# Four-layer graph stack: runs of three pairs of heads, a ring of row sums, and another close of each block in the multi-head layer

## The chip, the cores and the metric

The kernel runs on one core of a Trainium2 chip. The metric is the device time of one execution in microseconds. Before the change three runs took 3386.57, 3389.37 and 3391.87 us; the median is 3389.37.

## The reference

Four graph layers follow each other on 4096 nodes with 256 features. Each is a kind of masked attention, whose output is added to its input and normalised by row. `adj` is a 4096 x 4096 matrix of 0 and 1. The change touches only layer 1, the multi-head one:

```python
x = _layernorm(x + _L0_gnn_ref(x, adj, W, a))            # additive, 4 heads
x = _layernorm(x + _L1_gnn_ref(x, adj, Wq, bq, ...))     # multi-head, 4 heads of 64
x = _layernorm(x + _L2_gnn_ref(x, adj, W, a))            # additive, 1 head
x = _layernorm(x + _L3_gnn_ref(x, adj, Wq, Wk))          # cosine

def _L1_gnn_ref(x, edge, Wq, bq, Wk, bk, Wv, bv):
    q, k, v = (_split_heads(x @ W + b) for W, b in ...)  # 4 heads of 64
    mask = (edge.T.astype(jnp.float32) - 1.0) * 10000.0
    scores = jnp.einsum('hnd,hmd->hnm', q, k) / np.sqrt(64)
    attn = jax.nn.softmax(scores + mask[None], axis=-1)
    ctx = jnp.einsum('hnm,hmd->hnd', attn, v)
    return ctx.transpose(1, 0, 2).reshape(x.shape[0], 256)
```

So each head needs the products of its exponentials with V, and their sums over m (the row sums), by which the products are divided.

## The kernel before

Everything is in 32-bit floats, and X, the features, stays in SBUF. The four layers are written one after another; `multi_head_attention` (L276 to L427) is the second. It first makes kT, qT (features on partitions) and V (nodes on partitions), then works through 8 blocks b of 512 output nodes. In a block it goes through 32 tiles j of 128 source nodes. In a step the scores lie transposed: source nodes on partitions, 512 outputs along the free axis.

The four heads go in two pairs, c = 0 and 1; r is the head within a pair. The two heads of a pair lie on partitions 0 to 63 and 64 to 127 of kT and qT. `weights` (L348) does this for a j, for both pairs: two score matmuls (L361), each contracting over 64 rows of the PE array, into a PSUM tile p of two banks; the exponential on ScalarE in place (L363); the multiplication by the mask on VectorE into an SBUF tile `prob` (L365); and the addition of `prob` to a running sum `den` in SBUF (L372, L374). Pair 0 is added by GpSimd in part 0. Pair 1 is added by VectorE in part 1, but for every fourth j, which GpSimd adds in part 2. `sums` (L376) multiplies `prob` by V (L383): two matmuls a pair with 64 output columns each, which go to the two halves of the PE array and accumulate in a PSUM tile `acc` over all 32 j. After the last j `acc` is copied out as `accS`, one half by ScalarE (L387), one by VectorE (L388).

`outputs` (L390) closes a block: matmuls of `den` with one column of ones sum over the partitions (24 of them, L398), their reciprocals are taken (L401), `accS` is transposed back by eight transposes (L405), multiplied by the reciprocals (L407) and added to X (L412), and `row_stats` takes mean and variance of each row for the layer norm (L101, L102).

The order is written out by hand at L416 to L425: `weights` of a step, then `sums` of the step before it, and the close of a block after step j = 1 of the next one. The tile framework turns the accesses into semaphore waits and keeps each engine's queue in nearly that order. A tile of a pool comes free when the last reader of its buffer is done. [...]three tiles p of two banks (`mh_pz`) and one `acc` of two (`mh_pa`). The tiles of the close, for row sums and transposes, are taken from the same three buffers p. Masks come by SP's queue as 32-bit integers, four tiles j in a load of 1 MB, three buffers. There are four `prob` buffers.

Of the kernel before, what the change touches and what calls it, by code (L numbers as in the profile page):

```python
# [8 lines left out]
FP = mybir.dt.float32  # L9
BF = mybir.dt.bfloat16  # L10
I32 = mybir.dt.int32
AF = mybir.ActivationFunctionType
OP = mybir.AluOpType
AX = mybir.AxisListType
PSUM = bass.MemoryType.PSUM

P = 128
D = 256
KC = D // P
QB = 4  # L20
QW = QB * P
# [5 lines left out]
def kernel(  # L27
# [25 lines left out]
    nc = tc.nc  # L53
    N = x.shape[0]
    NT = N // P
    NB = N // QW
# [4 lines left out]
    ident = const.tile([P, P], FP, name="ident")  # L61
# [42 lines left out]
    def finish_stats():  # L104
        nc.scalar.activation(rstd, stats[:, :, 1], AF.Sqrt, bias=eps)
        nc.vector.reciprocal(rstd, rstd)

    def normalise(y, t):
        nc.vector.tensor_scalar(y, y, stats[:, t, 0:1], rstd[:, t:t + 1], OP.subtract, OP.mult)  # L109

    def layernorm():
        finish_stats()
        for t in range(NT):
            normalise(X[:, t, :D], t)


    def additive_attention(w, a_src, a_dst, H, slope):
# [4 lines left out]
        g = 1.0 - slope  # L122
        MJ = 4
        with ExitStack() as lay:
# [48 lines left out]
            def weights(b, j):  # L173
                m = b, j // MJ
                if j % MJ == 0:
                    mask[m] = mp.tile([P, MJ, QW], I32, name="mask")
                    nc.sync.dma_start(mask[m], edges[:, j:j + MJ, b * QW:(b + 1) * QW])
                e = sb.tile([P, H, QW], FP, name="e")
                for h in range(H):
                    nc.scalar.activation(e[:, h, :], row[b][:, h, :], AF.Relu, bias=-1.0, scale=dst[:, j, h:h + 1])  # L180
                z = prob[b, j] = zp.tile([P, H, QW], FP, name="prob")
                nc.vector.scalar_tensor_tensor(z, e, 1.0, mask[m][:, j % MJ, :].unsqueeze(1).to_broadcast([P, H, QW]),  # L182
                                               OP.add, OP.mult)
# [75 lines left out]
            units = [(b, j) for b in range(NB) for j in range(NT)]  # L259
            LAG = 1  # L260
            for i in range(len(units) + LAG):
                if i < len(units):
                    b, j = units[i]
                    weights(b, j)
                    if H > 1 and j == NT // 2 and b + 1 < NB:
                        rows(ps, b + 1)
                if i >= LAG:
                    b, j = units[i - LAG]
                    sums(b, j)
# [6 lines left out]
    def multi_head_attention():  # L276
# [2 lines left out]

        H = 4  # L280
        d = D // H
        MJ = 4
        with ExitStack() as lay:
            keep = lay.enter_context(tc.tile_pool(name="mh_keep", bufs=1))
            kT = keep.tile([P, KC, N], FP, name="kT")
            qT = keep.tile([P, KC, N], FP, name="qT")
            V = keep.tile([P, NT, D], FP, name="V")
            ones = keep.tile([P, P], FP, name="ones")
            nc.vector.memset(ones, 1.0)
            shift = keep.tile([P, 1], FP, name="shift")  # L290
            qscale = d ** -0.5

            with tc.tile_pool(name="mh_w", bufs=1) as wp, \
# [10 lines left out]
                for b in range(NB):  # L304
                    xT = transposed_block(sb, ps, b)
                    for n, to, scale in (("k", kT, 1.0), ("q", qT, qscale)):
                        for o in range(KC):
                            pk = ps.tile([P, QW], FP, name="pk")
                            for c in range(KC):
                                nc.tensor.matmul(pk, w_sb[n][:, c, o * P:(o + 1) * P], xT[:, c, :],  # L310
                                                 start=(c == 0), stop=(c == KC - 1))
                            part = to[:, o, b * QW:(b + 1) * QW]
# [3 lines left out]
                    for k in range(QB):  # L316
                        pv = ps.tile([P, D], FP, name="pv")
                        for c in range(KC):
                            nc.tensor.matmul(pv, xT[:, c, k * P:(k + 1) * P], w_sb["v"][:, c, :],
                                             start=(c == 0), stop=(c == KC - 1))  # L320
# [9 lines left out]
                for r in range(KC):  # L330
                    half = slice(r * d, (r + 1) * d)
# [4 lines left out]
                nc.vector.tensor_scalar(shift, shift, -1.0, ROOM, OP.mult, OP.add)  # L336
                nc.vector.tensor_scalar_min(shift, shift, 0.0)

            sb = lay.enter_context(tc.tile_pool(name="mh_sb", bufs=4))
            mp = lay.enter_context(tc.tile_pool(name="mh_mask", bufs=3))  # L340
            ap = lay.enter_context(tc.tile_pool(name="mh_acc", bufs=1))
            dp = lay.enter_context(tc.tile_pool(name="mh_den", bufs=2))
            ps = lay.enter_context(tc.tile_pool(name="mh_pz", bufs=3, space=PSUM))
            pa = lay.enter_context(tc.tile_pool(name="mh_pa", bufs=1, space=PSUM))
            edges = adj.rearrange("(t p) i -> p t i", p=P)
            mask, acc, prob, den = {}, {}, {}, {}

            def weights(u):  # L348
                b, j = u
                cols = slice(b * QW, (b + 1) * QW)  # L350
                m = b, j // MJ
                if j % MJ == 0:
                    mask[m] = mp.tile([P, MJ, QW], I32, name="mask")
                    nc.sync.dma_start(mask[m], edges[:, j:j + MJ, cols])
                if j == 0:
                    den[b] = dp.tile([P, 3, KC * QW], FP, name="den")
                for c in range(KC):
                    p = ps.tile([P, KC, QW], FP, name="p")
                    for r in range(KC):
                        half = slice(r * d, (r + 1) * d)  # L360
                        nc.tensor.matmul(p[:, r, :], kT[half, c, j * P:(j + 1) * P], qT[half, c, cols],  # L361
                                         start=True, stop=True)
                    nc.scalar.activation(p, p, AF.Exp, bias=shift)  # L363
                    z = prob[b, j, c] = sb.tile([P, KC, QW], FP, name="prob")
                    nc.vector.tensor_tensor(z, p, mask[m][:, j % MJ, :].unsqueeze(1).to_broadcast([P, KC, QW]),  # L365
                                            OP.mult)

                    part, eng = (0, nc.gpsimd) if c == 0 else (2, nc.gpsimd) if j % 4 == 3 else (1, nc.vector)
                    to = den[b][:, part, :]
                    flat = z.rearrange("p r i -> p (r i)")  # L370
                    if j == 0 or (part == 2 and j == 3):
                        eng.tensor_copy(to, flat)  # L372
                    else:
                        eng.tensor_tensor(to, to, flat, OP.add)  # L374

            def sums(u):  # L376
                b, j = u
                if j == 0:
                    acc[b] = pa.tile([P, KC, QW], FP, name="acc")
                for c in range(KC):  # L380
                    for r in range(KC):
                        h = KC * c + r
                        nc.tensor.matmul(acc[b][r * d:(r + 1) * d, c, :], V[:, j, h * d:(h + 1) * d],  # L383
                                         prob[b, j, c][:, r, :], start=(j == 0), stop=(j == NT - 1))
                if j == NT - 1:
                    s = acc[b, "sb"] = ap.tile([P, KC, QW], FP, name="accS")
                    nc.scalar.copy(s[:, 0, :], acc[b][:, 0, :])  # L387
                    nc.vector.tensor_copy(s[:, 1, :], acc[b][:, 1, :])  # L388

            def outputs(b):  # L390
                s = acc[b, "sb"]
                pd = ps.tile([P, QB, H], FP, name="p")
                for k in range(QB):
                    for h in range(H):
                        lo = (h % KC) * QW + k * P
                        parts = (0,) if h < KC else (1, 2)
                        for n in parts:
                            nc.tensor.matmul(pd[:, k, h:h + 1], den[b][:, n, lo:lo + P], ones[:, 0:1],  # L398
                                             start=(n == parts[0]), stop=(n == parts[-1]))
                rden = ap.tile([P, QB, H], FP, name="rden")  # L400
                nc.vector.reciprocal(rden, pd)  # L401
                po = ps.tile([P, QB, D], FP, name="p")
                for k in range(QB):
                    for c in range(KC):
                        nc.tensor.transpose(po[:, k, c * P:(c + 1) * P], s[:, c, k * P:(k + 1) * P], ident)  # L405
                o = ap.tile([P, QB, D], FP, name="o")
                nc.vector.tensor_tensor(o.rearrange("p k (h d) -> p (k h) d", h=H),  # L407
                                        po.rearrange("p k (h d) -> p (k h) d", h=H),
                                        rden.rearrange("p k h -> p (k h)").unsqueeze(2).to_broadcast([P, QB * H, d]),
                                        OP.mult)  # L410
                y = X[:, b * QB:(b + 1) * QB, :D]
                nc.vector.tensor_tensor(y, y, o, OP.add)  # L412
                for k in range(QB):
                    row_stats(sb, X[:, b * QB + k, :D], b * QB + k)

            units = [(b, j) for b in range(NB) for j in range(NT)]  # L416
            LAG = 1
            for i in range(len(units) + LAG):
                if i < len(units):
                    weights(units[i])  # L420
                if i >= LAG:
                    u = units[i - LAG]
                    sums(u)
                    if u[1] == 1 and u[0]:
                        outputs(u[0] - 1)  # L425
            outputs(NB - 1)
            layernorm()  # L427


# [139 lines left out]
```

## Time and profile before

| | us |
|---|---|
| median of three runs | 3389.37 |
| profiled execution | 3383.42 |
| its span | 3381.6 |
| multi-head layer, main loop, from the first L361 to the last L383 | 990.6 to 2043 |
| PE busy / VectorE / ScalarE / GpSimd over the span | 95% / 65% / 50% / 32% |
| in 1380 to 1500 us: PE / VectorE / ScalarE / GpSimd busy of 120 us | 118.8 / 104.2 / 59.4 / 96.7 |
| granted TensorE clock, mean | 0.976 |

A 32-bit matmul stands as two records in the trace, so an "x8" in the timeline is four matmuls of the program. Matmuls of different row or column groups of the PE array run at the same time. A row of a group gives the busy time and the mean of one instruction in ns; behind the second bar stands the idle time of the engine ahead of these instructions, and who ended it.

### The profile page before, as it was taken

The page shows a single profiled execution, that of the slowest core. Times are in us where ns is not written, and L with a number is a line of the kernel's source. Part 1 is how long each engine was busy: PE and PEld are TensorE (multiplying, and loading weights), DVE is VectorE, ACT ScalarE, POOL GpSimd, SP SyncE. Part 2 cuts the span into 40 slices and gives each one's busy share as a digit, 9 for nine tenths or more (in the row PEclk, how much of TensorE's full clock was granted, in tenths as well). Part 3 has the DMA queues.
Part 4 walks back from the last instruction along what each step waited for, and adds up shares of the span by engine and source line. Part 5 has one row for each costly group of instructions (what it writes and reads, how often), then busy time and mean ns, then how long its engine had stood idle before and what let it go on. Part 6 is the DMA issues. An engine that isn't in the chain of part 4 may idle for free. (4 is left out here: it accounts for less than half of the span.)

```text
span 3381.6 us, 37876 instructions
## 1 busy us (share of the span) xinstructions
PE 3226.4 (95%) x14596; PEld 1608.3 (48%) x14596; DVE 2201.5 (65%) x2738; ACT 1687.3 (50%) x2589; POOL 1067.1 (32%) x486
## 2 busy tenths in 40 slices
PE   7999999999799999999999997999997899999997
PEld 4222222222342332333333324788886677777775
DVE  4777887778559889888898895444545433333333
ACT  4888888888335455454454552444443422222221
POOL 0011111011019788797797892001101000000000
PEclk9999999999899999999999997999998999999998
DMA  3222222222101111121121111344442233333332
GB/s 106 88 88 75 88 88 76 87 88 75 49 13 63 63 63 64 62 75 63 51 74 63 63 50 44 112 144 142 143 144 78 37 51 50 50 50 50 51 52 60
DMA packets 146965, 247.93 MB, mean 73 GB/s; under 512 B 5344, under 2 KB 48480, under 8 KB 146784
## 3 DMA queue, kind: packets, MB, share of 16 engines
q1 hardware_dynamic: 109824, 209.73, 19.0%
q0 software_dynamic: 33280, 33.56, 6.5%
q8 instruction: 114, 1.87, 0.2%
q10 hardware_dynamic: 3680, 2.23, 0.2%
q14 instruction: 67, 0.55, 0.1%
HBM read 274.86 MB, written 4.19 MB: 83 GB/s over the span
## 5 line engine op out<-in xcount | busy, mean ns | idle before, releaser
L182 DVE SCALAR_TENSOR_TENSOR prob<-e,mask 128x2048 f32<-128x2048 f32 (+1 forms) x512 | 765.7, 1496 | 364.6 <-PE acc L215 213.5
L374 POOL TENSOR_TENSOR den<-den,prob 128x1024 f32<-128x1024 f32 x304 | 864.0, 2857 | 167.0 <-DVE prob L365 155.8
L363 ACT ACTIVATE p<-p,shift 128x1024 f32<-128x1024 f32 x512 | 537.6, 1085 | 501.7 <-PE p L361 501.7
L180 ACT ACTIVATE e<-row,dst 128x512 f32<-128x512 f32 x1024 | 657.7, 711 | 77.7 <-DVE prob L182 77.7
L365 DVE TENSOR_TENSOR prob<-p,mask 128x1024 f32<-128x1024 f32 x512 | 601.7, 1214 | 79.9 <-issue 67.3
L361 PE MATMUL p<-qT,kT 64*128 64x512 f32 x2048 | 523.2, 627 | 13.6 <-DVE prob L365 13.2
L238 PE MATMUL acc<-prob,V 128*64 128x512 f32 x2048 | 528.8, 608 | 0.0
L383 PE MATMUL acc<-prob,V 128*64 128x512 f32 x2048 | 496.7, 606 | 0.1
L491 PE MATMUL acc<-X,prob 128*128 128x257 f32 x2048 | 487.0, 382 | 4.0 <-DVE prob L484 4.0
L491 PEld LDWEIGHTS acc<-X,prob 128*128 128x128 f32 x2048 | 389.5, 191 | 165.5 <-issue 112.4
L215 PE MATMUL acc<-V,prob 128*128 128x257 f32 x2048 | 450.0, 381 | 18.0 <-DVE prob L182 17.0
L192 POOL TENSOR_SCALAR neg<-o 128x256 f32<-128x256 f32 x64 | 57.5, 899 | 1278.2 <-DVE o L189 753.3
L484 DVE TENSOR_TENSOR prob<-prob,mask 128x512 f32<-128x512 f32 x256 | 176.2, 691 | 437.2 <-ACT prob L483 427.2
L215 PEld LDWEIGHTS acc<-V,prob 128*128 128x128 f32 x2048 | 386.9, 190 | 80.9 <-DVE prob L182 25.5
L483 ACT ACTIVATE prob<-p 128x512 f32<-128x512 f32 x256 | 152.2, 597 | 513.4 <-PE p L480 464.6
L361 PEld LDWEIGHTS p<-qT,kT 64*128 64x128 f32 x2048 | 177.6, 189 | 347.8 <-issue 300.0
L374 DVE TENSOR_TENSOR den<-den,prob 128x1024 f32<-128x1024 f32 x184 | 301.8, 1640 | 6.1
L238 PEld LDWEIGHTS acc<-prob,V 128*64 128x64 f32 x2048 | 128.9, 136 | 354.2 <-issue 204.8
L180 ACT ACTIVATE e<-allrows,dst 128x512 f32<-128x512 f32 x256 | 184.1, 721 | 223.0 <-DVE prob L182 221.2
L383 PEld LDWEIGHTS acc<-prob,V 128*64 128x64 f32 x2048 | 124.3, 136 | 344.2 <-issue 321.5
L241 PE MATMUL acc<-prob,V 128*32 128x512 f32 x2048 | 278.9, 604 | 0.0
L480 PE MATMUL p<-kT,qT 128*128 128x512 f32 x512 | 259.6, 592 | 0.7 <-ACT kT L465 0.7
(111 smaller groups left out, 1549.2 us busy)
## 6 DMA issues: line engine op xcount, KB each, us to landing
mask<-in_adjT SPq DMA_DIRECT2D x128, 1024.0 KB, 5.2
mask<-in_adj SPq DMA_DIRECT2D x64, 1024.0 KB, 5.2
mask<-in_adjT POOLq DMA_DIRECT2D x32, 1024.0 KB, 8.5
X<-in_x SPq DMA_DIRECT2D x8, 512.0 KB, 9.5
out<-Y SPq DMA_DIRECT2D x8, 512.0 KB, 4.0
w_sb<-in_w ACTq DMA_DIRECT2D x2, 256.0 KB, 4.9
a<-in_a ACTq DMA_DIRECT2D x4, 128.0 KB, 8.0
wq_sb<-in_wq ACTq DMA_DIRECT2D x1, 256.0 KB, 2.7
```

The source lines that it names most:

```text
L180: nc.scalar.activation(e[:, h, :], row[b][:, h, :], AF.Relu, bias=-1.0, scale=dst[:, j, h:h + 1])
L182: nc.vector.scalar_tensor_tensor(z, e, 1.0, mask[m][:, j % MJ, :].unsqueeze(1).to_broadcast([P, H, QW]), OP.add, OP.mult)
L215: nc.tensor.matmul(acc[b][k], prob[b, j][:, 0, k * P:(k + 1) * P], V[:, j, :], start=(j == 0), stop=(j == NT - 1))
L238: nc.tensor.matmul(acc[b][lo:lo + d, h // 2, :], V[:, j, h * d:(h + 1) * d], prob[b, j][:, h, :], start=(j == 0), stop=(j == NT - 1))
L241: nc.tensor.matmul(acc[b][h * G:(h + 1) * G, HC, :], V[:, j, D + h:D + h + 1].to_broadcast([P, G]), prob[b, j][:, h, :], start=(j == 0), s ...
L361: nc.tensor.matmul(p[:, r, :], kT[half, c, j * P:(j + 1) * P], qT[half, c, cols], start=True, stop=True)
L363: nc.scalar.activation(p, p, AF.Exp, bias=shift)
L365: nc.vector.tensor_tensor(z, p, mask[m][:, j % MJ, :].unsqueeze(1).to_broadcast([P, KC, QW]), OP.mult)
L374: eng.tensor_tensor(to, to, flat, OP.add)
L383: nc.tensor.matmul(acc[b][r * d:(r + 1) * d, c, :], V[:, j, h * d:(h + 1) * d], prob[b, j, c][:, r, :], start=(j == 0), stop=(j == NT - 1))
L480: nc.tensor.matmul(p, T["q"][:, j * P:(j + 1) * P], T["k"][:, cols], start=True, stop=True)
L491: nc.tensor.matmul(acc[b][k], prob[u][:, k * P:(k + 1) * P], X[:, j, :], start=(j == 0), stop=(j == NT - 1))
```

## The change

Only `multi_head_attention` changes.

- The unit of the order is now one pair (b, j, c) instead of both pairs of a j. Units go in runs of three: scores of three units, then sums of the three units of the run before, so that PE changes between scores and sums after six matmuls of the program instead of four.
- The row sums: pair 0, and pair 1 of odd j, are added by GpSimd to the two parts of `den`. Pair 1 of even j is not added one by one: its `prob` is written into a slot of a ring tile with three slots. After j = 2, 6, 10, ... one VectorE `tensor_reduce` sums the slots into slot 0 of the next ring tile (two buffers). Slot 0 carries the sum, and slots 1 and 2 take the next two units.
- The close: the row sums over partitions are now six matmuls with 32 output columns and 512 elements each, a group of 32 partitions for each head, copied out by ScalarE (`denS`) and transposed by four transposes. The result of the division goes into `accS` again instead of a tile of its own. It comes after the sums of unit j = 2 of the next block, and the row statistics only after j = 6. Both halves of `accS` are copied by ScalarE.
- Buffers: masks come two tiles j in a load (512 KB) instead of four, `prob` has five buffers, and a tile of the pool `mh_sb` two.

```diff
@@ -279,7 +279,7 @@
         H = 4
         d = D // H
-        MJ = 4
+        MJ = 2
         with ExitStack() as lay:
             keep = lay.enter_context(tc.tile_pool(name="mh_keep", bufs=1))
             kT = keep.tile([P, KC, N], FP, name="kT")
@@ -336,94 +336,121 @@
                 nc.vector.tensor_scalar(shift, shift, -1.0, ROOM, OP.mult, OP.add)
                 nc.vector.tensor_scalar_min(shift, shift, 0.0)
-            sb = lay.enter_context(tc.tile_pool(name="mh_sb", bufs=4))
+            sb = lay.enter_context(tc.tile_pool(name="mh_sb", bufs=2))
+            zp = lay.enter_context(tc.tile_pool(name="mh_z", bufs=5))
+            rp = lay.enter_context(tc.tile_pool(name="mh_ring", bufs=2))
             mp = lay.enter_context(tc.tile_pool(name="mh_mask", bufs=3))
             ap = lay.enter_context(tc.tile_pool(name="mh_acc", bufs=1))
             dp = lay.enter_context(tc.tile_pool(name="mh_den", bufs=2))
             ps = lay.enter_context(tc.tile_pool(name="mh_pz", bufs=3, space=PSUM))
             pa = lay.enter_context(tc.tile_pool(name="mh_pa", bufs=1, space=PSUM))
             edges = adj.rearrange("(t p) i -> p t i", p=P)
-            mask, acc, prob, den = {}, {}, {}, {}
-
-            def weights(u):
-                b, j = u
+            mask, acc, prob, den, ring = {}, {}, {}, {}, {}
+            W = KC * QW
+            RJ = 4
+            def weights(b, j, c):
                 cols = slice(b * QW, (b + 1) * QW)
                 m = b, j // MJ
-                if j % MJ == 0:
+                if c == 0 and j % MJ == 0:
                     mask[m] = mp.tile([P, MJ, QW], I32, name="mask")
                     nc.sync.dma_start(mask[m], edges[:, j:j + MJ, cols])
-                if j == 0:
-                    den[b] = dp.tile([P, 3, KC * QW], FP, name="den")
-                for c in range(KC):
-                    p = ps.tile([P, KC, QW], FP, name="p")
-                    for r in range(KC):
-                        half = slice(r * d, (r + 1) * d)
-                        nc.tensor.matmul(p[:, r, :], kT[half, c, j * P:(j + 1) * P], qT[half, c, cols],
-                                         start=True, stop=True)
-                    nc.scalar.activation(p, p, AF.Exp, bias=shift)
-                    z = prob[b, j, c] = sb.tile([P, KC, QW], FP, name="prob")
-                    nc.vector.tensor_tensor(z, p, mask[m][:, j % MJ, :].unsqueeze(1).to_broadcast([P, KC, QW]),
-                                            OP.mult)
-
-                    part, eng = (0, nc.gpsimd) if c == 0 else (2, nc.gpsimd) if j % 4 == 3 else (1, nc.vector)
-                    to = den[b][:, part, :]
+                if c == 0 and j == 0:
+                    den[b] = dp.tile([P, 2, W], FP, name="den")
+                p = ps.tile([P, KC, QW], FP, name="p")
+                for r in range(KC):
+                    half = slice(r * d, (r + 1) * d)
+                    nc.tensor.matmul(p[:, r, :], kT[half, c, j * P:(j + 1) * P], qT[half, c, cols],
+                                     start=True, stop=True)
+                nc.scalar.activation(p, p, AF.Exp, bias=shift)
+                ringed = c == 1 and j % 2 == 0
+                if ringed:
+                    if j == 0:
+                        ring[b, 0] = rp.tile([P, 3, W], FP, name="ring")
+                    flat = ring[b, j // RJ][:, 1 + (j % RJ) // 2, :]
+                    z = flat.rearrange("p (r i) -> p r i", r=KC)
+                else:
+                    z = zp.tile([P, KC, QW], FP, name="prob")
                     flat = z.rearrange("p r i -> p (r i)")
-                    if j == 0 or (part == 2 and j == 3):
-                        eng.tensor_copy(to, flat)
+                prob[b, j, c] = z
+                nc.vector.tensor_tensor(z, p, mask[m][:, j % MJ, :].unsqueeze(1).to_broadcast([P, KC, QW]),
+                                        OP.mult)
+                if not ringed:
+                    to = den[b][:, c, :]
+                    if j == c:
+                        nc.gpsimd.tensor_copy(to, flat)
                     else:
-                        eng.tensor_tensor(to, to, flat, OP.add)
-
-            def sums(u):
-                b, j = u
-                if j == 0:
+                        nc.gpsimd.tensor_tensor(to, to, flat, OP.add)
+                elif j % RJ == 2:
+                    this = ring[b, j // RJ]
+                    nxt = rp.tile([P, 3, W], FP, name="ring")
+                    ring[b, j // RJ + 1] = nxt
+                    lo = 1 if j == 2 else 0
+                    nc.vector.tensor_reduce(nxt[:, 0, :], this[:, lo:, :].rearrange("p s f -> p f s"), AX.X, OP.add)
+            def sums(b, j, c):
+                if c == 0 and j == 0:
                     acc[b] = pa.tile([P, KC, QW], FP, name="acc")
-                for c in range(KC):
-                    for r in range(KC):
-                        h = KC * c + r
-                        nc.tensor.matmul(acc[b][r * d:(r + 1) * d, c, :], V[:, j, h * d:(h + 1) * d],
-                                         prob[b, j, c][:, r, :], start=(j == 0), stop=(j == NT - 1))
+                for r in range(KC):
+                    h = KC * c + r
+                    nc.tensor.matmul(acc[b][r * d:(r + 1) * d, c, :], V[:, j, h * d:(h + 1) * d],
+                                     prob[b, j, c][:, r, :], start=(j == 0), stop=(j == NT - 1))
                 if j == NT - 1:
-                    s = acc[b, "sb"] = ap.tile([P, KC, QW], FP, name="accS")
-                    nc.scalar.copy(s[:, 0, :], acc[b][:, 0, :])
-                    nc.vector.tensor_copy(s[:, 1, :], acc[b][:, 1, :])
+                    if c == 0:
+                        acc[b, "sb"] = ap.tile([P, KC, QW], FP, name="accS")
+                    nc.scalar.copy(acc[b, "sb"][:, c, :], acc[b][:, c, :])
             def outputs(b):
+                G = P // H
                 s = acc[b, "sb"]
-                pd = ps.tile([P, QB, H], FP, name="p")
+                last = ring[b, NT // RJ][:, 0, :]
+                pd = ps.tile([P, KC, QW], FP, name="p")
+                for h in range(H):
+                    cols = slice((h % KC) * QW, (h % KC + 1) * QW)
+                    parts = [den[b][:, h // KC, cols]] + ([last[:, cols]] if h >= KC else [])
+                    for n, part in enumerate(parts):
+                        nc.tensor.matmul(pd[h * G:(h + 1) * G, 0, :], ones[:, :G], part,
+                                         start=(n == 0), stop=(n == len(parts) - 1))
+                denS = ap.tile([P, QW], FP, name="denS")
+                nc.scalar.copy(denS, pd[:, 0, :])
                 for k in range(QB):
-                    for h in range(H):
-                        lo = (h % KC) * QW + k * P
-                        parts = (0,) if h < KC else (1, 2)
-                        for n in parts:
-                            nc.tensor.matmul(pd[:, k, h:h + 1], den[b][:, n, lo:lo + P], ones[:, 0:1],
-                                             start=(n == parts[0]), stop=(n == parts[-1]))
-                rden = ap.tile([P, QB, H], FP, name="rden")
-                nc.vector.reciprocal(rden, pd)
+                    nc.tensor.transpose(pd[:, 1, k * P:(k + 1) * P], denS[:, k * P:(k + 1) * P], ident)
+                rden = ap.tile([P, QB * H], FP, name="rden")
+                nc.vector.reciprocal(rden, pd[:, 1, ::G])
                 po = ps.tile([P, QB, D], FP, name="p")
                 for k in range(QB):
                     for c in range(KC):
                         nc.tensor.transpose(po[:, k, c * P:(c + 1) * P], s[:, c, k * P:(k + 1) * P], ident)
-                o = ap.tile([P, QB, D], FP, name="o")
-                nc.vector.tensor_tensor(o.rearrange("p k (h d) -> p (k h) d", h=H),
+                nc.vector.tensor_tensor(s.rearrange("p c (k h d) -> p (c k h) d", h=H, d=d),
                                         po.rearrange("p k (h d) -> p (k h) d", h=H),
-                                        rden.rearrange("p k h -> p (k h)").unsqueeze(2).to_broadcast([P, QB * H, d]),
-                                        OP.mult)
+                                        rden.unsqueeze(2).to_broadcast([P, QB * H, d]), OP.mult)
                 y = X[:, b * QB:(b + 1) * QB, :D]
-                nc.vector.tensor_tensor(y, y, o, OP.add)
+                nc.vector.tensor_tensor(y, y, s.rearrange("p c (k f) -> p (c k) f", f=D), OP.add)
+            def close(b):
                 for k in range(QB):
                     row_stats(sb, X[:, b * QB + k, :D], b * QB + k)
-            units = [(b, j) for b in range(NB) for j in range(NT)]
-            LAG = 1
-            for i in range(len(units) + LAG):
-                if i < len(units):
-                    weights(units[i])
-                if i >= LAG:
-                    u = units[i - LAG]
-                    sums(u)
-                    if u[1] == 1 and u[0]:
-                        outputs(u[0] - 1)
+            units = [(b, j, c) for b in range(NB) for j in range(NT) for c in range(KC)]
+            RUN = 3
+            groups = [units[i:i + RUN] for i in range(0, len(units), RUN)]
+            for i in range(len(groups) + 1):
+                if i < len(groups):
+                    for u in groups[i]:
+                        weights(*u)
+                if i:
+                    for u in groups[i - 1]:
+                        sums(*u)
+                        if u[0] and u[2]:
+                            if u[1] == 2:
+                                outputs(u[0] - 1)
+                            elif u[1] == 6:
+                                close(u[0] - 1)
             outputs(NB - 1)
+            close(NB - 1)
             layernorm()
```

## The prediction

> **What bounds the kernel now.** I read the page first: the 40 slices show PE at 9 almost everywhere, and between about 985 and 2060 us VectorE (DVE) at 8 or 9 and GpSimd (POOL) at 7 to 9. That stretch is the multi-head layer, the only one touched. Its rows, from the groups of instructions in 985 to 2050 us (the last line in the same view up to 985 us):
>
> ```profile
> L374 POOL TENSOR_TENSOR den<-den,prob 128x1024 f32<-128x1024 f32 x304 | 864.0, 2857 | 167.0 <-DVE prob L365 155.8
> L365 DVE TENSOR_TENSOR prob<-p,mask 128x1024 f32<-128x1024 f32 x512 | 601.7, 1214 | 79.9 <-issue 67.3 <-ACT p L363 9.5
> L361 PE MATMUL p<-qT,kT 64*128 64x512 f32 x2048 | 523.2, 627 | 13.6 <-DVE prob L365 13.2 <-DVE most L334 0.3
> L374 DVE TENSOR_TENSOR den<-den,prob 128x1024 f32<-128x1024 f32 x184 | 301.8, 1640 | 6.1
> ...
> L314 DVE TENSOR_REDUCE kbig<-kT 128x1 f32<-128x512 f32 x16 | 11.0, 686 | 31.4 <-ACT kT L313 31.4
> ```
>
> PE waits for DVE only 13.2 us in all at L361 (its weight loads, which run ahead, 40.4), so PE sets the pace. How, the timeline of PE, ACT and DVE inside a block tells:
>
> ```profile
> 1202.95 1.99 PE L361 MATMUL p<-qT,kT 64*128 64x512 f32 x8
> 1204.87 1.94 PE L383 MATMUL acc<-prob,V 128*64 128x512 f32 x8
> 1206.74 1.99 PE L361 MATMUL p<-qT,kT 64*128 64x512 f32 x8
> ...
> 1204.13 2.09 ACT L363 ACTIVATE p<-p,shift 128x1024 f32<-128x1024 f32 x2 [1.69 <-PE p L361]
> ...
> 1205.31 2.36 DVE L365 TENSOR_TENSOR prob<-p,mask 128x1024 f32<-128x1024 f32 x2 [1.42 <-issue]
> ```
>
> One j (two pairs of heads) takes 1206.74 - 1202.95 = 3.79 us, 1.92 of it scores, 1.87 sums. Inside such a stretch the weight loads follow each other every 0.43 us, and four of these (1.71) are the work of two pairs; so each change between scores and sums costs 0.21 or 0.16 us, 0.37 a turn. Read also: the exponential starts 1.18 us after its scores' stretch, the multiplication 2.36 us after it.
>
> The close of a block, from the full timeline:
>
> ```profile
> 1127.18 6.03 PE L398 MATMUL p<-ones,den 128*128 128x1 f32 x48
> 1132.86 1.76 PEld L405 LDWEIGHTS p<-ident,accS 128*128 128x128 f32 x8
> 1134.94 3.79 PE L361 MATMUL p<-qT,kT 64*128 64x512 f32 x8
> 1138.66 2.00 PE L383 MATMUL acc<-prob,V 128*64 128x512 f32 x8
> 1140.59 1.99 PE L361 MATMUL p<-qT,kT 64*128 64x512 f32 x8
> ```
>
> From 1127.18 to 1140.59 there are 13.41 us with one j in them: the close costs 9.62, of which 1.8 is the score stretch at half speed (3.79 for 1.99). The copies at L387 run from 1119.73 to 2043.92: seven blocks of 132.03 us, which is 32 x 3.79 = 121.3, the 9.6, and 1.1 of other waits. The first block, 990.55 to 1119.7, has 129.2. Early in it DVE's adds and POOL's get in each other's way: in the timeline a den add on DVE takes 2.42 us when it lies under a POOL add, 1.23 when not.
>
> **What the Trainium skill says.** "TensorEngine Tiling (Array Packing)", Tiling Modes (Key Properties): changing the tiling mode drains the array. The 0.37 us a turn agrees. "VectorE: DVE Perf Modes", the perf-mode tier table: tensor_reduce runs at one element a cycle only. L314 agrees: 512 elements in 686 ns, 0.96 GHz and 153 ns fixed. "SBUF — State Buffer", Who interferes with whom: a DVE instruction with two SBUF inputs contends with GpSimd, one with a single SBUF input does not. The 2.42 against 1.23 us agrees, as does L365 (one input in PSUM), never above 1.226. The same page, Specifications: SBUF lines have 16 bytes, and full bandwidth needs two hits a line. The new reduce reads its addends 4 KB apart, one hit a line. No row of before has such a read, so this stays open.
>
> **The change, part by part.** The sum stands against the profiled execution, 3383.4 us with a span of 3381.6; the median of the runs is 6 higher.
>
> 1. *Runs of three.* 256 turns of 3.79 become 170.7 turns of 6 x 0.853 + 0.37 = 5.49. A block falls from 121.3 to 117.1: -4.2.
>
> 2. *The adds.* POOL gets 46 adds and 2 copies a block where it had 38 and 2. Without DVE's two-input adds beside it an add is the median 2.37 us, so 46 x 2.37 + 2 x 1.04 = 111 us of a block of over 130. It keeps up; five prob buffers, with six of eight units using them, allow it about two turns of lag. No cost.
>
> 3. *The reduce.* It takes three addends, 3072 elements: 3072/0.96 + 153 = 3.35 us, eight times a block (the first with two, 2.29). In amount this is no more than three adds of 1.23. But it is one piece, and it stands in DVE's order directly behind the multiplication of its unit. Behind it wait the multiplications of the rest of the run, and these free the PSUM buffers p: there are three, and a run of three fills all of them, so scores k of a run need the multiplication k of the run before. Take a run whose scores start at 0. Exponentials are ready for multiplication at 2.36, 3.4, 4.4. Multiplications of 1.21, one each 1.14, end at 3.57, 4.70, 5.85. The next scores start at 5.49 and need the second buffer by 6.35, the third by 7.20 (at 1016.40 a load of the second pair, 1.24 us into the stretch of 1015.16, put its end off by 0.38, so it is due at 0.86). Without a reduce there is more than a microsecond of slack.
>    - Reduce behind the first: 3.61 to 6.96; multiplications end 8.10 and 9.24. PE loses 1.81, then 0.28: 2.1.
>    - Behind the second: 4.74 to 8.09, third multiplication ends 9.23: 2.1 lost.
>    - Behind the third: 5.89 to 9.24; the next run's multiplications end 10.4, 11.5, 12.65, due 11.0, 11.8, 12.7: nothing lost.
>
>    A reduce comes every 8 units, and 8 mod 3 is 2, so all three places are equally frequent: 1.4 us a reduce, seven a block, +9.8.
>
> 4. *The close.* Six 32-column products in place of 24 with one column. The rows of L241 show four of that kind side by side in 1.0 us; here two heads have two parts each, so three rounds: 2.7. Then the copy on ACT, 0.59, and twelve transposes of 0.22. New is a wait: the ring's first reduce in a block overwrites the buffer that the old block's products read, so it waits for them, and behind it stands a multiplication that frees the buffer of the transposes. From the scores' start at 0: products 3.8 to 6.5, reduce 6.6 to 8.8, multiplication to 10.0, eight transposes to 12.0, the sums left over to 14.6, where next scores start instead of at about 5.9: +8.7. Both accS copies are now on ACT, the second behind three exponentials: about 0.7 of waiting, and a split score pair adds one turn, 0.4. Together 9.8 a block, where before had 9.6 + 1.1. I take no half-speed stretch here; one would cost 1.8 more. bn statistics move to j = 6 and lie in DVE's slack: 2.2 us a block, nothing if away from a reduce.
>
> 5. *Masks.* 128 loads of 512 KB for 64 of 1 MB on SP, whose queue holds nothing else here. They are asked for four j ahead, over 14 us, and a 1 MB load landed in 5.2. Nothing.
>
> Blocks 2 to 8: 117.1 + 9.8 + 9.8 = 136.7 for 132.0, +4.7, seven times +33. First block: 117.1 + 9.8 + 2.5 of filling the pipeline for 129.2, zero. After the last sums, before waited 15.1 us until L407 (2043.9 to 2059.0); I count POOL 2, products 2.7, copy 0.8, transposes 2.9, and as much as double at half speed: -4. Sum +29: 3412 for the profiled execution, **3418** against the median.
>
> **Rivals.**
> - *Lines.* The reduce reads one hit a line and needs two cycles an element: 6144/0.96 + 153 = 6.55 us. The same schedule then loses 5.3, 5.3 and 3.2, 4.6 on average: 56 x (4.6 - 1.4) = +179, and 2 more for each of seven closes. 3418 + 193 = 3611. For it the skill's line rule; against it that L327, with a stride of 8 bytes, shows no surcharge (16 elements in 158 to 170 ns), though that has two hits a line.
> - *The close is worth more.* If the transposes do not queue behind the reduce and the clock holds, it is products, copy, transposes and switches, about 5.5 instead of 9.8: 3418 - 30 = 3388, no difference to speak of.
> - *Faster: the reduce is absorbed.* Place: the buffers of p. If a reduce took two elements a cycle, 1.75 us, it would lose 0.33 on average instead of 1.4: 3418 - 60 = 3358. It decides at about 2.6 us a reduce, where 0.88 us of loss each leaves nothing of the 29. L314 at one element a cycle speaks against it.
>
> **How the numbers follow.** About 0.2% (7 us; the three runs span 5) can be told from no change. My case 0.55 (3400 to 3445: the close may be 2.5 off each time), lines 0.27, close 0.10, absorbed 0.08. The range runs from 3385, in the close's case, to 3635, past the lines' case. Faster: absorbed and 0.04 of the close, 0.12. Same: 0.05. Slower: the rest, 0.83.
>
> **What would show it.** Right: the gap from scores to scores 5.49 where no reduce lies, and about 2.1 us of PE waiting for DVE at the score line after two reduces of three; tensor_reduce near 3.35 us; POOL adds near 2.37. Wrong: a reduce far from 3.35 us, waits of PE under 40 us in all at the score line, POOL adds still near 2.9, or a score line at half speed for long.

## The result, and the profile after

Four runs of the changed kernel took 3426.35 to 3431.52 us, with a median of 3430.31; four of the kernel before, on the same chip, had a median of 3389.60. The ratio is 1.0119, with a 95% interval of 1.0101 to 1.0136: slower by some 41 us, where the forecast was slower by 29. The profiled execution took 3431.52 us, with a span of 3429.7 and a mean granted clock of 0.974.

The groups of instructions on the page of the kernel after. A line gives the count, then busy time and the mean of one in ns, then idle time ahead of these instructions and what ended it:

```profile
L385 POOL TENSOR_TENSOR den<-den,prob 128x1024 f32<-128x1024 f32 x368 | 859.1, 2362 | 229.5 <-DVE prob L378 198.4
L365 PE MATMUL p<-qT,kT 64*128 64x512 f32 x2048 | 530.1, 629 | 77.8 <-DVE prob L378 76.7
L378 DVE TENSOR_TENSOR prob<-p,mask 128x1024 f32<-128x1024 f32 x384 | 450.7, 1216 | 183.1 <-ACT p L367 140.7
L391 DVE TENSOR_REDUCE ring<-ring 128x1024 f32<-128x3072 f32 (+1 forms) x64 | 224.4, 3506 | 9.5 <-PE p L414 7.6
```

L365 is the score line (L361 before), L378 the multiplication by the mask, L385 the adds, L391 the new reduce. GpSimd's adds are at their undisturbed 2.36 us. What has grown is the second line: before, PE waited for VectorE 13.2 us at the scores, now 76.7.

More work on VectorE is not the reason. These two lines are the main loop of the layer, first before, then after, from the view of busy times by stretch:

```profile
990.50:2043.90 1053.40, 1039.91 (x4488) 355.13 (x4488) 932.26 (x791) 542.98 (x520) 880.07 (x319) 0.98 0.19 61
```

```profile
990.50:2103.00 1112.50, 1033.06 (x4267) 326.46 (x4268) 849.60 (x656) 548.62 (x536) 874.73 (x384) 0.97 0.19 60
```

After the stretch and its length come the busy times of PE, PE's weight loads, VectorE, ScalarE and GpSimd, each with its count; the granted clock, the DMA share and GB/s end the line. VectorE has 83 us less to do, GpSimd 5 less, PE 7 less. Yet the stretch is 59 us longer. After it come 11 us of gain: from the end of the last sums to the multiplication by the reciprocals (L426, before L407) in the layer's last block, 4 us pass where before it was 15.1.

How the time goes, the timeline of PE and of VectorE shows for one reduce of the kernel after:

```profile
1070.59 3.68 DVE L391 TENSOR_REDUCE ring<-ring 128x1024 f32<-128x3072 f32 x1
1074.17 3.48 DVE L378 TENSOR_TENSOR prob<-p,mask 128x1024 f32<-128x1024 f32 x3
...
1071.34 1.99 PE L365 MATMUL p<-qT,kT 64*128 64x512 f32 x8
1075.45 1.13 PE L365 MATMUL p<-qT,kT 64*128 64x512 f32 x4 [2.12 <-DVE prob L378]
1076.51 1.08 PE L398 MATMUL acc<-prob,V 128*64 128x512 f32 x4
```

The reduce starts after two multiplications of its run. The third waits behind it until 1074.17 and ends at 1075.3. Meanwhile PE has done the scores of two pairs, needs the third buffer p, and gets it 2.12 us late. From the first score to the first sum 5.17 us pass; an undisturbed run has 2.78, so 2.39 are lost. Behind the first multiplication of a run (the reduce at 2077.82 in the same kernel's timeline) the loss is 2.33. Behind the third, the two runs take 5.50 and 5.79 instead of 5.5 each: 0.29 lost. Up to 1250 us every reduce away from a close, but for the very first, shows one of these three, the first two at times with what the next lines show on top.

Often more than the stall is lost. The PE timeline of the kernel after, 100 us later:

```profile
1175.64 1.99 PE L365 MATMUL p<-qT,kT 64*128 64x512 f32 x8
1179.74 1.69 PE L365 MATMUL p<-qT,kT 64*128 64x512 f32 x4 [2.12 <-DVE prob L378]
1181.36 1.98 PE L398 MATMUL acc<-prob,V 128*64 128x512 f32 x4
```

It is the same stall of 2.12 us, but after it four records take 1.69 and 1.98 us instead of 1.13 and 1.08. From scores to scores 92 of 178 intervals are 5.5 us; 16 are 7.7 to 8.0, which is the stall alone; 15 are 9.4 to 9.6, which is the stall and about 1.6 more. The trace's records of the granted clock have 19 stretches of 3.41 us at half speed inside the loop, 64.8 us together. Before there were eight with 44.4 us together, all at the starts of blocks. The stretch behind the loop, 37.6 us from 2046.8 on before, now has 23.9 us and starts only when PE is through with the close (2108.6).

Which stalls bring half speed can be read from these records. The starts of the 19 stretches lie whole multiples of 3.413 us apart: 995.85, 1023.16, 1043.64 and 1094.84, for instance, by 8, 6 and 15 of them. If the loop is cut into slices at these distances, each of the 19 follows a slice in which PE waited 1.7 us or more. The stall shown last lies whole in the slice from 1176.76 to 1180.17, and half speed starts at 1180.17. The one shown before it is cut by the border at 1074.36 into 1.03 and 1.09 us, and nothing follows. Of the slices with 1.7 us or more of waiting, four (1.78 to 1.82 us) have no half speed behind them, so the bound is not sharp. This is read from the two kinds of records side by side; no run varied it.

Last, the close of a block, from the full timeline of the kernel after:

```profile
1145.89 1.07 PE L414 MATMUL p<-den,ones 128*32 128x512 f32 x8
1146.79 1.03 PE L414 MATMUL p<-ring,ones 128*32 128x512 f32 x4
...
1147.88 2.32 DVE L391 TENSOR_REDUCE ring<-ring 128x1024 f32<-128x2048 f32 x1 [0.17 <-PE p L414]
...
1148.76 0.65 PE L419 MATMUL p<-ident,denS 128*128 128x128 f32 x4
...
1149.25 1.04 PE L425 MATMUL p<-ident,accS 128*128 128x128 f32 x8
```

The six products take 1.86 us (1145.89 to 1147.75). The ring's first reduce waits for them, as foreseen. But the eight transposes of L425 run during this reduce, not after it.

### The profile page after: what moved, and what is told of

Its sections match the earlier page's. It is cut to its first block, busy times and chain, and to the rows that moved or that the text cites. A ratio compares the mean times of both kernels' runs of the same rounds, so it can differ in the third digit from the quotient of the medians.

```text
span 3429.7 us, 37508 instructions
## 1 busy us (share of the span) xinstructions
PE 3213.1 (94%) x14340; PEld 1570.5 (46%) x14340; DVE 2118.8 (62%) x2602; ACT 1693.6 (49%) x2605; POOL 1059.0 (31%) x550
## 5 line engine op out<-in xcount | busy, mean ns | idle before, releaser
L385 POOL TENSOR_TENSOR den<-den,prob 128x1024 f32<-128x1024 f32 x368 | 859.1, 2362 | 229.5 <-DVE prob L378 198.4
L365 PE MATMUL p<-qT,kT 64*128 64x512 f32 x2048 | 530.1, 629 | 77.8 <-DVE prob L378 76.7
L378 DVE TENSOR_TENSOR prob<-p,mask 128x1024 f32<-128x1024 f32 x384 | 450.7, 1216 | 183.1 <-ACT p L367 140.7
L238 PE MATMUL acc<-prob,V 128*64 128x512 f32 x2048 | 528.9, 608 | 0.0
L398 PE MATMUL acc<-prob,V 128*64 128x512 f32 x1536 | 390.9, 614 | 0.5 <-DVE prob L378 0.5
L365 PEld LDWEIGHTS p<-qT,kT 64*128 64x128 f32 x2048 | 178.4, 187 | 414.6 <-DVE prob L378 233.2
L238 PEld LDWEIGHTS acc<-prob,V 128*64 128x64 f32 x2048 | 129.0, 136 | 354.9 <-issue 206.5
L505 POOL DMA_DIRECT2D mask<-in_adjT x32 | 28.3, 884 | 659.5 <-DVE prob L511 578.5
L391 DVE TENSOR_REDUCE ring<-ring 128x1024 f32<-128x3072 f32 (+1 forms) x64 | 224.4, 3506 | 9.5 <-PE p L414 7.6
```

The source lines that it names most:

```text
L238: nc.tensor.matmul(acc[b][lo:lo + d, h // 2, :], V[:, j, h * d:(h + 1) * d], prob[b, j][:, h, :], start=(j == 0), stop=(j == NT - 1))
L385: nc.gpsimd.tensor_tensor(to, to, flat, OP.add)
```

## The experiments

The theory: the reduce stands in VectorE's order ahead of multiplications that free the buffers of p, and its place is what costs, not its amount. Two rivals stood against it: the reduce is too much work for VectorE; or the cost lies in runs of three themselves, which fill all buffers of p. A further question was whether the sum came near only because a wrongly priced close made up for something else.

**Without the reduce.** The slots of the ring are written as before, but nothing sums them. Left out of the row sums is most of pair 1 in even j.

```diff
-                    lo = 1 if j == 2 else 0
-                    nc.vector.tensor_reduce(nxt[:, 0, :], this[:, lo:, :].rearrange("p s f -> p f s"), AX.X, OP.add)
...
-                last = ring[b, NT // RJ][:, 0, :]
+                last = ring[b, NT // RJ - 1][:, 2, :]
```

> The changed kernel without its 64 reduces, so most of pair 1's even j is missing from the row sums; the closing matmuls stay six. Theory, that a reduce standing ahead of multiplications holds up the scores and that PE then also loses half-speed stretches: 37 stalls of 2.35 us and some 36 us of half speed go, so 3290 to 3315 us, and PE's wait for VectorE at the score line falls from 77 us to under 25. Rival, that runs of three are too tight for three buffers p by themselves: above 3400 us, with the waits still there.

It took 3303.18 us, ratio to the kernel before 0.9750 (0.9730 to 0.9769). The reduces cost 127 us, while their busy time is 224. The score line of this kernel, from the groups of its layer:

```profile
L365 PE MATMUL p<-qT,kT 64*128 64x512 f32 x2048 | 496.3, 609 | 3.5 <-DVE prob L378 3.1 <-DVE most L334 0.3
```

The wait is gone, and of the 19 half-speed stretches in the loop one is left. A block takes 122.4 us, where after has 138.4: a reduce costs 2.0 us there.

**The same reduces behind the last multiplication of their run.** The work is the same as in the changed kernel; a reduce is only held back until the run's three multiplications are in the queue. It is pinned there in program order.

```diff
-                    nc.vector.tensor_reduce(nxt[:, 0, :], this[:, lo:, :].rearrange("p s f -> p f s"), AX.X, OP.add)
+                    late.append((nxt[:, 0, :], this[:, lo:, :]))
...
                         weights(*u)
+                    while late:
+                        to, parts = late.pop()
+                        tc.keep_in_program_order(
+                            nc.vector.tensor_reduce(to, parts.rearrange("p s f -> p f s"), AX.X, OP.add))
```

> Each reduce is issued behind the last multiplication of its run; the amount of work is the same. Theory (place in the queue): the third place lost next to nothing, with 3.68 us a reduce some 0.3 us each, so 3310 to 3345 us and few half-speed stretches. Rival (amount of VectorE work): no change, 3420 to 3440 us.

It took 3321.08 us, ratio 0.9804 (0.9789 to 0.9818). Its groups:

```profile
L366 PE MATMUL p<-qT,kT 64*128 64x512 f32 x2048 | 507.5, 615 | 6.9 <-DVE prob L379 5.9 <-DVE accS L427 0.4 <-DVE most L334 0.3
L448 DVE TENSOR_REDUCE ring<-ring 128x1024 f32<-128x3072 f32 (+1 forms) x64 | 224.0, 3500 | 8.2 <-PE p L415 7.6
```

The same 64 reduces take the same 224 us, and PE waits 5.9 us instead of 76.7. In the timeline of VectorE and PE, around a reduce that in the changed kernel stood in the middle of its run:

```profile
1062.49 1.22 DVE L379 TENSOR_TENSOR prob<-p,mask 128x1024 f32<-128x1024 f32 x1
1063.62 3.66 DVE L448 TENSOR_REDUCE ring<-ring 128x1024 f32<-128x3072 f32 x1
1067.20 2.34 DVE L379 TENSOR_TENSOR prob<-p,mask 128x1024 f32<-128x1024 f32 x2
...
1063.36 2.85 PE L366 MATMUL p<-qT,kT 64*128 64x512 f32 x12
1066.14 1.08 PE L399 MATMUL acc<-prob,V 128*64 128x512 f32 x4
...
1068.86 3.00 PE L366 MATMUL p<-qT,kT 64*128 64x512 f32 x12
```

The reduce lies beside the next scores, which already have their buffers. The run after it starts on time, 5.50 us later, and its scores take 3.00 us for 2.85. So of the 127 us that the reduces cost, 109 (3430.3 - 3321.1) are their place in the queue; 18 are left at the ends of runs. This decides against the amount of work, and together with the experiment before it against runs of three: both kernels have them, and next to no wait.

**Runs of three and the new close, with the adds as before.** No ring; pair 1 is added by VectorE in three j of four, as before the change, and `prob` has eight buffers.

```diff
+                part, eng = (0, nc.gpsimd) if c == 0 else (2, nc.gpsimd) if j % 4 == 3 else (1, nc.vector)
+                to = den[b][:, part, :]
...
+                    eng.tensor_tensor(to, to, flat, OP.add)
```

> Runs of three and the new close, but row sums by adds on VectorE and GpSimd as in the kernel before, with eight prob buffers. Theory: an add is 1.23 us alone and up to 2.4 us under a GpSimd add, so one piece is shorter than a reduce and stalls are smaller, but GpSimd and VectorE contend again: 3340 to 3400 us. Rival (runs of three too tight): 3430 us or more.

It took 3427.43 us (3422.75 to 3442.50), ratio 1.0124 (1.0099 to 1.0149). That is outside what the theory expected, and just below the 3430 from which the rival's range began; one of the four runs lies in it. The expectation missed. Its groups:

```profile
L364 PE MATMUL p<-qT,kT 64*128 64x512 f32 x2048 | 548.2, 632 | 80.9 <-DVE prob L368 76.8 <-DVE most L334 0.3
L376 DVE TENSOR_TENSOR den<-den,prob 128x1024 f32<-128x1024 f32 x184 | 424.5, 2307 | 6.2
```

An add of VectorE takes 2.31 us on the mean, where before it was 1.64. Before, 102 of the 184 took the undisturbed 1.2 us; here 31 do, 71 take 2.3 to 2.4, and 44 take 3.0 to 3.4. The rival's number nearly came out, but its mechanism, the runs themselves, does not hold: the two experiments above have runs of three and nearly no wait. Whether the adds cost by their place or by their amount is not separated here. VectorE is busy for 1062.9 of the loop's 1122.9 us, 95%, where the kernel with reduces at run ends has 842 of 1001; a kernel with these adds at the ends of runs was not made. What the traces do show in favour of the ring is that its reduce and GpSimd's adds leave each other alone: GpSimd's adds take 2.36 us with the reduces and without them.

**The new close alone.** The kernel before, with only the close of the changed one (the six products, `denS`, the later places of close and statistics, both copies on ScalarE).

```diff
-                    nc.vector.tensor_copy(s[:, 1, :], acc[b][:, 1, :])
+                    nc.scalar.copy(s[:, 1, :], acc[b][:, 1, :])
...
+                        nc.tensor.matmul(pd[h * G:(h + 1) * G, 0, :], ones[:, :G], part,
...
-                    if u[1] == 1 and u[0]:
+                    if u[1] == 2 and u[0]:
                         outputs(u[0] - 1)
+                    elif u[1] == 6 and u[0]:
+                        close(u[0] - 1)
```

> The kernel before with the new close alone (six column-tiled matmuls, transposes, both accS copies on ScalarE, statistics after j = 6). From the changed kernel's trace the close costs about 6 us a block instead of 9.6 to 10.7 and the tail 10 us less: 3335 to 3365 us. If the close costs what the prediction said, 9.8 us a block: 3380 to 3390 us.

It took 3347.26 us, ratio 0.9880 (0.9863 to 0.9896). A block takes 128.1 us for 132.0. So the new close is worth 3.9 us a block, where the prediction had priced both closes about alike; by that price this kernel would have come to 3380 or more.

Most of this is clock. Before, each of blocks 2 to 8 has a stretch at half speed, 41.0 us in all, and each begins while PE works off the 24 one-column products: those of the first close run from 1127.18 to 1133.2, and half speed starts at 1132.01. In this kernel, whose products have 512 elements, none of the seven is left. At half speed 41.0 us lose about 20.5, an estimate of 2.9 of the 3.9 us a block. That the one-column products bring these stretches rests on this coincidence; the parts of the new close were not tried one by one.

**Half reduces.** A whole reduce at the end of a run still delays the next run a little. Here six of the eight of a block are cut into two of 512 outputs each, behind successive runs; the block's first and last stay whole. It starts from the version with reduces at run ends.

```diff
-                    late.append((nxt[:, 0, :], this[:, lo:, :]))
+                    for half in [slice(0, W)] if j in (2, NT - 2) else [slice(0, QW), slice(QW, W)]:
+                        late.append((nxt[:, 0, half], this[:, lo:, half]))
...
-                    while late:
-                        to, parts = late.pop()
+                    if late:
+                        to, parts = late.pop(0)
```

> Reduces at run ends as in the run before, but each (save the first and the last of a block) cut in two halves of 512 outputs, about 1.9 us each, behind two runs that follow each other. A run has 5.5 us for three multiplications (3.5) and a half. Theory (length of one piece ahead of multiplications): nothing is left to stall, 3303 to 3315 us, close to the kernel without reduces (3303). If what is left between 3321 and 3303 is the amount of VectorE work: 3318 us or more, the halves having more fixed cost.

It took 3309.39 us (3308.94 to 3310.10), ratio 0.9763 (0.9749 to 0.9778): faster than the kernels before and after, and 6 us above the one that leaves the reduces out. (The last three experiments ran on another chip than the first four; the kernel before took 2 us more there.) Its score line:

```profile
L366 PE MATMUL p<-qT,kT 64*128 64x512 f32 x2048 | 499.0, 610 | 4.1 <-DVE prob L379 3.1 <-DVE accS L428 0.4 <-DVE most L334 0.3
```

VectorE spends more on these 112 reduces than on the 64 (231 us for 224), and the kernel is 12 us faster. So most of the 18 us left at run ends was not amount either: again the piece that stands ahead of a multiplication counts, not the sum.

**What a reduce costs by its form.** The reduce had 3.67 us where 3.35 was reckoned. After the layer, on a tile of the ring, eight reduces were put one after another, with different distances and numbers of addends.

```diff
             close(NB - 1)
+            probe = rp.tile([P, 3, W], FP, name="ring")
...
+            for view in (probe.rearrange("p s f -> p f s"),
+                         flat.rearrange("p (f s) -> p f s", s=3),
...
+                nc.vector.tensor_reduce(scrap[:, :view.shape[1]], view, AX.X, OP.add)
```

> Eight reduces of known form behind the layer's close, which change nothing of the output; the time is 15 to 30 us longer and not of interest. Which of two readings explains 3674 ns with three addends and 2316 with two: if addends far apart cost extra, three neighbouring addends take 3353 ns and three 4 KB apart 3674; if a reduce of three costs extra per output whatever the distance, both take 3674, and four, five, six and twelve addends tell how it goes on.

From the timeline of VectorE in this kernel, three addends for each output, first 4 KB apart, then neighbours:

```profile
1992.70 3.68 DVE L471 TENSOR_REDUCE prob<-ring 128x1024 f32<-128x3072 f32 x1
1996.68 3.30 DVE L471 TENSOR_REDUCE prob<-ring 128x1024 f32<-128x3072 f32 x1
```

And the groups by form; the mean of one in ns stands after the comma:

```profile
L471 DVE TENSOR_REDUCE prob<-ring 128x768 f32<-128x3072 f32 x1 | 5.3, 5318 | 0.0
L471 DVE TENSOR_REDUCE prob<-ring 128x512 f32<-128x3072 f32 x1 | 5.3, 5294 | 0.0
L471 DVE TENSOR_REDUCE prob<-ring 128x1024 f32<-128x2048 f32 x2 | 4.6, 2289 | 0.0
```

Neighbouring addends come within 2% of the reckoned 3.35. Distance costs 0.38 us with three addends and nothing with two (2.30 us 4 KB apart, 2.28 as neighbours, together in the last line). Four addends 3 KB apart (768 outputs) and six 2 KB apart (512) take 2.0 us more than three neighbours for the same 3072 elements; four or six neighbours were not measured. So the distance is what makes the ring's reduce longer than reckoned. A surcharge for distance, as the rival "lines" supposed, exists, but for a reduce of three it is small, and none of these forms reaches that rival's 6.55 us. Each form was measured once.

**Runs of two.** The kernel without reduces, in runs of two instead of three.

```diff
-            RUN = 3
+            RUN = 2
```

> The kernel without reduces (most of pair 1's even j missing from the row sums), but in runs of two: 85 more turns between scores and sums. Theory (0.37 us a turn): 3303 + 32, so 3328 to 3342 us. If longer runs save nothing once the stalls are gone: 3300 to 3310 us.

It took 3327.16 us (3326.76 to 3328.30), a microsecond below what was expected. So runs of three are worth some 24 us (22 if the difference of the two chips is taken off), or 3.3 a block (125.7 for 122.4) instead of 4.2. An interval from scores to scores is 3.8 us here and 5.5 in the other, as reckoned; what is missing lies outside these intervals, at block ends and closes: 5.3 us a block with runs of three, 4.4 with runs of two.

## Why the prediction was right

The direction was right, and so were the mechanism that makes the kernel slower and its place: reduces ahead of multiplications that free the buffers p. 3418 against 3430.31 is 12 low. Against the profiled execution it is 3412 for 3431.5, of which blocks 2 to 8 account for +12 (138.4 us from the second copy of `acc` to the next one, instead of 136.7), the first block for +14 (143.6 instead of 129.4), and the tail for -7. But inside a block two wrong terms nearly cancel, the reduces priced too low and the close too high, so that the sum came this near is luck.

1. *Runs of three*: 5.49 expected, 5.5 measured; worth 3.3 a block instead of 4.2.
2. *The adds*: right. 2.36 us each; VectorE's multiplications waited 13.7 us for GpSimd's adds in the whole layer.
3. *The reduce*: right in kind. Two places of three stall PE, by 2.33 and 2.39 us for the 2.1 expected, and the third by 0.29. It was under-priced twice. It takes 3.67 us instead of 3.35, and that is due to the distance of its addends. And its stalls bring stretches at half speed, which the prediction had named as a sign against itself and not counted. With eight reduces a block at (2.33 + 2.39 + 0.29) / 3 = 1.67 us, stalls come to an estimated 13.4 us; the 18 half-speed stretches more than with the reduces at run ends, at half of 3.41 us each, to 31 us in the layer, or 3.9 a block. Together 17, and leaving out the reduces saved 16.0, where 9.8 were expected. The first block has this cost too: it took 127 us with the reduces at run ends, 143.6 here, and so the "zero" expected of it fell.
4. *The close*: the mechanism was wrong, not only the size. It was to cost 9.8 us a block, because the transposes of `accS` were to queue behind the ring's first reduce. In the timeline they run during it: their buffer was freed by a multiplication ahead of the reduce. The products take 1.86 us instead of 2.7, and a transpose about 0.11 instead of 0.22: the clock is full here, where the row that the 0.22 came from lies in a stretch at half speed (before, 1132.01 to 1138.84). Without reduces a block is 122.4 us, of which 117.1 are runs: 5.3 for the close, near the 5.5 that the rival "the close is worth more" gave. The tail gained more too, -11 instead of -4: its first product runs ahead of the last sums (from 2100.85), and the rest of the close at full clock.
5. *Masks*: right; 3.7 us a load, and no wait on them.

So the rival of the close was right about its step, and alone would have ended at 3388; the half-speed stretches (31 us), the longer reduce and its stalls took this back. Seen against the kernel before, the change exchanged one kind of half speed for another: 41.0 us at the closes for 61.4 behind the reduces' stalls. (Both have one more stretch of 3.41 us as the loop begins.) "Lines" fell with the reduce at 3.67 instead of 6.55 us. "Absorbed" fell as well: PE waits 76.7 us. Pieces that are absorbed exist, but they need the other place too: half reduces of 1.90 us at the ends of runs, in the kernel that is 80 us faster than the one before.

The Trainium skill's "VectorE: DVE Perf Modes", perf-mode tier table (tensor_reduce at one element a cycle), held for neighbouring addends (3.30 us for 3072 elements). "SBUF — State Buffer", Specifications, asks for two hits a line for full bandwidth. Of the reads measured here with one hit a line, those with four and more addends are slower (5.3 us), those with two addends 4 KB apart are not (2.30 us, no surcharge), so the rule alone does not give the cost: there the measurement decides.

What stays open: stall and half speed were not tried apart. That the stretches at half speed follow from the stalls of the scores rests on their coming right after them, in the slices of 3.413 us described above, and on their leaving when the reduces are moved or taken out; a kernel with the stalls and without the half speed was not made. Nor was the ring compared with plain adds at the ends of runs.

## What to carry to other kernels

Ask of a long instruction in an in-order queue not how much it adds but what stands behind it and which buffers that frees. The same 224 us of reduces cost 127 us where two of three stood inside a run, and 18 at the ends of runs; cut mostly in halves there, 231 us of them cost 6. In this kernel a run fills all three buffers p, and a piece of 3.67 us does not fit inside it; the slack is behind its last multiplication. So try side work there first, in pieces shorter than that slack.

## What had not been expected of the hardware

Waits of TensorE of only about 2 us were followed by stretches of 3.41 us at half clock, 19 of them in the loop; with the same work and 5.9 us of score waits for VectorE in all there was one. Whether a wait of this length brought one went with where it fell: the 19 starts lie on one raster of 3.413 us, and each follows a slice of it with 1.7 us or more of waiting. And a tensor_reduce over addends far apart changes its pace with their number: 2.30 us for two 4 KB apart (2048 elements), 3.68 for three 4 KB apart, 5.3 for four 3 KB or six 2 KB apart (3072 elements each).
